# Moving attention scores inside a feed-forward unit of a two-layer graph network, with a new order of work at both ends

## The chip, the cores and the metric

The kernel runs on one core of a Trainium2 chip, in fp32. A core has TensorE for matrix products (PE in the profile; its weight loads are PEld), VectorE (DVE), ScalarE (ACT), GpSimd (POOL) and SyncE (SP), which here only issues transfers. Each engine works through its own queue in order. SBUF holds the data; TensorE writes its results to PSUM, from where VectorE and ScalarE read them. The metric is the time of the device in microseconds (us), lower is better. [...]

## What is computed

The input is x with 128 batches of 128 tokens by 256 features, and for each batch an adjacency matrix of zeros and ones. Two layers follow each other. Cut to what matters:

```python
# layer 0: attention with 8 heads, values chosen by the relation adj == r
attn = softmax(q @ k.T / sqrt(32))
out  = sum(attn * (adj == r) @ (src @ Wv[r]) for r in range(4))
x    = ln(src + out @ Wo)
x    = ln(x + gelu(x @ W1) @ W2)
# layer 1: two graph attention steps
def gat(h, W, a):
    Wh = h @ W
    e = leaky_relu(Wh @ a[:256] + (Wh @ a[256:]).T, 0.2)
    return softmax(where(adj > 0, e, -9e15), axis=1) @ Wh
h = ln(x + gat(gat(x, W1, a1), W2, a2))
h = ln(h + relu(h @ w_ff1) @ w_ff2)
```

Since adj holds only zeros and ones, the kernel needs two value projections: all exponentials times the values of relation 0, plus the exponentials that the adjacency leaves times the difference of the values of relation 1 and 0. Sums that it keeps on the way are checked at the end; if the check fails, a general pass repeats the work. It does not run here.

## The kernel before

**Groups.** The 128 batches are worked on in 32 groups of four (512 tokens). The loop over groups is software-pipelined: in iteration g the kernel is in the first feed-forward of group g+1, in the graph layer and the second feed-forward of group g, in the attention of group g+2 and in the projections of groups g+2 and g+3.

**Products.** The projections and the feed-forwards use a form of the 2x2 block product that needs seven products in place of eight. They are called B11, B21, B22 and T1 to T4; the sums of weights that they need are made once, by `combined` (L184), and those of the data by VectorE (`turned`, L389 to L392). A feed-forward (`ffn`) makes the hidden activations in two units, r=0 and r=1. In each, TensorE does T3, T2, B21, T1, T4, then B11 of the next unit if there is one, then B22, each four matmuls of L411. Products that share a sum accumulate in the same PSUM bank: `seeded` is held throughout and takes T2, T1 and B22 in turn, with what ScalarE or VectorE must read in between. So after T1 VectorE's addition L466 reads `seeded`, and B22 can only be written once it has. ScalarE applies GELU or ReLU (L435). Then follow the seven products with the second matrix, sixteen matmuls of L420 each: po1 (B11, copied to `seeded` by L498), po7 (T3), T2, B21, T1, T4 and B22. The projections (`projected`, products L641) use the banks `qa` and `qb`.

**Attention.** `scores` makes one pair of batches: 32 matmuls of 32 rows (L709) into four banks, for the first pair in the order `qa`, `qb` and the two banks of `ps_s`, and four exponentials of ScalarE (L715) that empty them. `masked` multiplies them with the adjacency on VectorE (L725). `sums` makes the denominators (`pden`, L742) and the value sums (`pav`, L756); ScalarE and VectorE turn them into `oT` (L766 to L778); `output` applies Wo (L791) and adds to x (`added`, L327).

**Graph layer.** `layer1` makes `wh` (L875), spreads one column of it over all partitions (`spread`: a transpose, and a write to HBM that is read back by all partitions, L838 and L839; for the first and last groups by matmuls, L828), and `edges` makes the weights `gs`: sums on ScalarE (L847), the leaky slope on VectorE (L851), exponentials (L853), adjacency and sums (L857), scaling (L864). Then come the products `py` (L888), the same once more, and `pg2` (L901).

**The order.** Nothing is scheduled by a planner. All stages are Python generators that `yield` between steps, and `in_order(...)` steps them: `(f1, 2)` takes two steps of the first feed-forward. Inside `tc.manual_schedule` every engine executes its instructions in the order in which they were written by these steps, and waits for what an instruction needs. In the lists f1 and f2 are the two feed-forwards, l1 the graph layer, at the attention, pr the projections, n0 to n3 the layer norms, `exp` and `gelu` the loads of ScalarE's function tables, `ahead` and `turned` the transposes. There are lists for the front (groups 0 and 1), for g=0, for the steady loop (g from 1, with small differences in the last iteration) and for the tail (the last group).

Of the kernel before, what the change touches and what calls it, by code (L numbers as in the profile page):

```python
# [10 lines left out]
F32 = mybir.dt.float32  # L11
# [13 lines left out]
P = 128  # L25
# [82 lines left out]
def fast_pass(ctx, tc, a, out):  # L108
# [73 lines left out]
    def combined(w):  # L182
        for o, p, q in ((T3, B22, T1), (T1, T1, B11), (T2, B22, T1), (T4, B21, T2)):
            nc.vector.tensor_sub(w[:, o], w[:, p], w[:, q])  # L184
# [508 lines left out]
    def scores(S, p):  # L693

        qT, kT = S["qT"], S["kT"]
        n = f"{S['g']}_{p}"


        banks = ((ps_1, "qa"), (ps_1, "qb"), (ps_s, "s"), (ps_s, "s"))
        pss = [  # L700
            pool.tile([P, 2, NCH, P], F32, tag=t, name=f"ps_{n}_{s}")
            for s, (pool, t) in enumerate(banks if p == 0 and S["g"] > 1 else banks[2:] + banks[:2])
        ]
        for u in range(2):
            bs = slice((2 * p + u) * P, (2 * p + u + 1) * P)
            for c in range(NCH):
                for s in range(HC):
                    rs = slice(s * DH, (s + 1) * DH)
                    nc.tensor.matmul(  # L709
                        pss[s][:, u, c, :], kT[rs, c, bs], qT[rs, c, bs],  # L710
                        start=True, stop=True,
                    )
        S["e", p] = e = w1p.tile([P, HC, 2, NCH, P], F32, tag="e", name="e_" + n)
        for s in range(HC):
            nc.scalar.activation(e[:, s], pss[s], AF.Exp, scale=SCALE)  # L715
            if s == 1:
                yield

    def masked(S, p):
# [10 lines left out]
    def sums(S, p):  # L730


        e, pm = S["e", p], S["pm", p]
        n = f"{S['g']}_{p}"

        pool, tag = (ps_1, "fe") if S["g"] > 1 and p == 0 else (ps_s, "s")
        pden = pool.tile([P, 2, NCH, P], F32, tag=tag, name="pden_" + n)
        pav = ps_1.tile([P, 2, NCH, P], F32, tag="av", name="pav_" + n)

        def plain():  # L740
            for s in range(HC):
                nc.tensor.matmul(  # L742
                    pden[s * DH : (s + 1) * DH], k.ones, e[:, s], start=True, stop=True
                )


        late = S["g"] > 1
        if not late:
            plain()
        for u in range(2):  # L750
            v = S["v"][:, 2 * p + u]
            for c in range(NCH):
                for r, m in enumerate((e, pm)):
                    for s in range(HC):
                        d0 = r * D + c * P + s * DH
                        nc.tensor.matmul(  # L756
                            pav[s * DH : (s + 1) * DH, u, c, :],
                            v[:, d0 : d0 + DH], m[:, s, u, c, :],
                            start=(r == 0), stop=(r == 1),
                        )  # L760
        if late:
            plain()

        g, oT = S["g"], S["oT"]
        rd = w1p.tile([P, 2, NCH, P], F32, tag="rd", name="rd_" + n)
        nc.scalar.activation(  # L766
            rd, pden, AF.Identity, accum_out=c_att[:, 1, g, p : p + 1]
        )
        nc.scalar.activation(
            pden, pden, AF.Relu, bias=k.lo, scale=-1.0, accum_out=c_att[:, 0, g, p : p + 1]  # L770
        )
        yield
        nc.vector.reciprocal(rd[:, 0], rd[:, 0])
        yield
        nc.vector.reciprocal(rd[:, 1], rd[:, 1])
        for u in range(2):
            bs = slice((2 * p + u) * P, (2 * p + u + 1) * P)
            nc.vector.tensor_mul(oT[:, :, bs], pav[:, u], rd[:, u])  # L778
        yield

    def attention(S):

        n = str(S["g"])
        S["oT"] = oT = w1p.tile([P, NCH, T], F32, tag="oT", name="oT_" + n)

        def output(p):
            po = mm_tile(f"pwo_{n}_{p}")
            for s in range(2):
                b = 2 * p + s
                for c in range(NCH):  # L790
                    nc.tensor.matmul(  # L791
                        po[:, s * D : (s + 1) * D], oT[:, c, b * P : (b + 1) * P], wo[:, c, :],
                        start=(c == 0), stop=(c == NCH - 1),
                    )
            added(S, 0, p, po)

        for p in range(G // 2):
            late = S["g"] > 1
            if p == 0 or not late:
                parts = scores(S, p)  # L800
                next(parts)
                if p == 0:
                    yield
                next(parts, None)
                yield
            masked(S, p)
            yield
            rest = sums(S, p)
            next(rest)
            yield  # L810
            if p == 0 and late:
                parts = scores(S, 1)
                next(parts)
                yield
                next(parts, None)
                yield
            yield from rest
        for p in range(G // 2):
            output(p)
            yield  # L820
# [87 lines left out]
    def store(S, bs=slice(0, G)):  # L908
        t0 = S["g"] * T
        nc.sync.dma_start(  # L910
            out[t0 + bs.start * P : t0 + bs.stop * P, :].rearrange("(b p) d -> p b d", p=P),
            S["x"][:, bs],
        )
# [23 lines left out]
    with tc.manual_schedule(engines={ET.PE, ET.Activation, ET.DVE, ET.SP, ET.Pool}):  # L937
# [11 lines left out]
        def output_bias():  # L949
# [7 lines left out]
            prepared(first)  # L957

        in_order(
            (pr, 4), (at, 2), (pr, 2), at, (pr, 2), (at, 4), (pr1, 2),  # L960
            at, output_bias, at, (pr1, 2), (at, 3), pr1, at, (at1, 2), n0, n0, lambda: combined(w1), pr1, at1, lambda: turned(first, 0), (at1, 2),
        )
        f1 = first_ffn(first)
        prepared(S1)
        st[2] = entered(2)
        pr = projected(st[2])
        in_order(
            gelu, (f1, 4), lambda: combined(w2), pr1, f1, f1, at1, at1, f1, lambda: combined(wqk), pr1, lambda: combined(wv), f1, n0, at1, (f1, 2), n0, f1, at1,
            (f1, 3), gwu, at1, f1, gwu, f1, at1, gwu,
            f1, at1, f1, gwu, at1, f1, n0_, pr, n0_, (f1, 4), n1_, (pr, 5), lambda: turned(S1, 0),  # L970
        )
        for g in range(NG - 1):
            S, S1 = st[g], st[g + 1]
# [9 lines left out]
            if g == 0:  # L983
                l1 = layer1(S)
                in_order(
                    f1, n1_, lambda: combined(u1), lambda: combined(u2), (pr, 2), (f1, 3), lambda: turned(S, 1), (pr, 2), f1, (n0_, 2), f1, l1, f1, (n1_, 2), l1, l1, f1, l1,
                    (f1, 2), (l1, 2), (pr, 2), f1, l1, (pr, 2), f1, pr, l1, f1, l1, f1, (l1, 2), exp, f1, (at, 2), (l1, 2),
                )
            else:
                n3 = norm(st[g - 1], 3)  # L990
                in_order(
                    pr, lambda: turned(S1, 0), (pr, 2), *(() if more else (f2_,)), f1, l1, gelu, (pr, 2), f2_, n3, f1, l1, pr,
                    n0_, f1, (pr, 2), (f1, 3), n0_, l1, f1, (pr, 2), l1, f1, n3, (pr, 2), f1, l1, f1, n3, (pr, 2),
                    (f1, 3), n3, lambda: store(st[g - 1]), f1, (n1_, 2), exp, (at, 2), f1, (l1, 3),
                )
            in_order(
                f1, (pr, 2), l1, f1, (pr, 2), at, f1, (pr, 2), l1, n2, (pr, 2), f1, n2, (pr, 2), f1, (pr, 2), f1, (pr, 2), *((ahead,) if more else ()), (at, 2), f1, n1,
                *(() if more else (ahead,)),
            )
            if not more:  # L1000
# [12 lines left out]
        in_order(f2, n1, (f2, 2), lambda: turned(S1, 1))  # L1013
        l1 = layer1(S1)
        in_order(
            f2, l1, f2, (l1, 2), f2, l1, (f2, 2), (l1, 2), n1, (f2, 2), l1, n1, f2, l1, f2, l1, f2, l1, n2, f2, (l1, 3), n2,
            (f2, 3), l1, (f2, 2), l1,
        )
        n2, n3 = norm(S1, 2), norm(S, 3)
        in_order(n2, f2, n2, (f2, 3), lambda: turned(S1, 2))  # L1020
        f2 = second_ffn(S1)
        in_order(f2, n3, (f2, 3), n2, n3, (f2, 4), n2, n3, (f2, 4), n3, lambda: store(S), (f2, 2))
        checks()
# [3 lines left out]
        normed(S1, 3, pair(1))  # L1027
        in_order(f2)
        root(S1, 3, pair(0))
        for p in (1, 0):  # L1030
            if p == 0:
                normed(S1, 3, pair(0))
            for step in range(2):
                scaled(S1, 3, step, (p,))
            store(S1, pair(p))

    same = flat(w1p.tile([P, G, P], F32, tag="gs", name="same"))[:, : NG * G * 2]
    fin = c_out.rearrange("p g b s -> p (g b s)")  # L1040
    nc.vector.tensor_tensor(same, fin, fin, op=ALU.is_equal)
    good = k.tile([P, 3], "good")
    nc.vector.tensor_reduce(good[:, 0:1], same, AX.X, ALU.min)
    nc.vector.tensor_reduce(good[:, 1:2], ok, AX.X, ALU.min)
    nc.vector.tensor_mul(good[:, 2:3], good[:, 0:1], good[:, 1:2])
    pf = mm_tile("pflag")
    nc.tensor.matmul(pf[:1, :1], good[:, 2:3], k.ones[:, 0:1], start=True, stop=True)
    bad = k.tile([1, 1], "bad", I32)
# [332 lines left out]
```

## Time and profile before

The median of three runs is 2760.3 us (2760.15 to 2761.74); the profiled span is 2759.6 us.

| engine | busy us | share of the span | instructions |
|---|---|---|---|
| PE | 2717.9 | 98% | 21621 |
| PEld (overlaps PE) | 2374.0 | 86% | 21621 |
| DVE | 2285.9 | 83% | 5320 |
| ACT | 1608.6 | 58% | 3589 |
| POOL | 135.9 | 5% | 137 |

The page has this table, the chain of work that ended last and the costliest groups of instructions. The windows view gives for a stretch of time its length, the busy time and count of each engine, the TensorE clock that was granted (PEclk, 1.00 is full), the share of the transfer engines and GB/s. A line of the timeline view gives the start in us, the duration, the engine, the line of code, the operation, the tile written, the tiles read, the shapes and how many instructions are joined in the line; in square brackets stands how long the engine had been idle, and what released it. Matmuls overlap, so a line of sixteen matmuls has a duration somewhat longer than its distance to the next start. The repeating part has a period of 82.8 us.

### The profile page before, as it was taken

Reading aid. Unit: us, or ns where it says so; the run is one execution under the profiler, and the core shown is the slowest. Engines: PE = TensorE matmul, PEld = TensorE weight load, DVE = VectorE, ACT = ScalarE, POOL = GpSimd, SP = SyncE. Lnnn points to the kernel's source line nnn. Section 1 sums busy time; section 2 is a strip of 40 time slices with the busy share of each in tenths; the row PEclk is TensorE's granted clock in tenths of the full one; section 3 lists DMA queues with packets and bytes.
Section 4 is the critical chain, followed back from the end, with each engine's and each line's share of the span. In section 5 each row is a group of like instructions: output and inputs, shape, how many; then the busy total and the mean of one; then the engine's idle time right before and its main releaser. Section 6 shows DMA issues by size and latency. Waiting matters only on the chain.

```text
span 2759.6 us, 54205 instructions
## 1 busy us (share of the span) xinstructions
PE 2717.9 (98%) x21621; PEld 2374.0 (86%) x21621; DVE 2285.9 (83%) x5320; ACT 1608.6 (58%) x3589; POOL 135.9 (5%) x137
## 2 busy tenths in 40 slices
PE   8899999999999999999999999999999999999997
PEld 5788898888888888888888888888888889888876
DVE  5778888888888888888888888888888888888866
ACT  4556656556556556565566565565665665655653
POOL 0000000000000000000000000000000000000000
PEclk9999999999999999999999999999999999999999
DMA  6001010010101010100101010101001101001000
GB/s 178 1 24 36 32 35 17 24 36 32 36 16 35 25 35 32 35 16 24 36 32 36 17 34 24 36 32 36 16 28 32 36 32 31 21 24 36 13 12 17
DMA packets 70234, 86.12 MB, mean 31 GB/s; under 512 B 8428, under 2 KB 48728, under 8 KB 69976
## 3 DMA queue, kind: packets, MB, share of 16 engines
q1 hardware_dynamic: 68872, 82.20, 9.6%
q8 instruction: 172, 2.82, 0.4%
q14 instruction: 86, 0.70, 0.1%
q10 hardware_dynamic: 1104, 0.40, 0.1%
HBM read 65.68 MB, written 16.90 MB: 30 GB/s over the span
## 4 chain that ended last, share of the span: by engine, by line
PE 94%; DVE 3%; ACT 2%; issue 0%; POOL 0%; ACTq 0%; POOLq 0%; DVEq 0%
PE po L420 16%; PE ph L411 15%; PE seeded L411 13%; PE seeded L420 12%; PE pav L756 4%; PE pwo L791 4%; PE pw L875 4%; PE pqqa L641 4%; PE pvqa L641 4%; PE pt L300 3%; PE pvqb L641 3%; PE pqqb L641 3%; PE ps L709 3%; PE py L888 2%; PE pden L742 2%; PE pg L901 2%
## 5 line engine op out<-in xcount | busy, mean ns | idle before, releaser
L349 ACT ACTIVATE x<-x,sh,rs 128x256 f32<-128x256 f32 x388 | 202.9, 608 | 425.8 <-DVE sh L344 425.8
L335 POOL TENSOR_TENSOR rs<-rs,mhalf 128x4 f32<-128x4 f32 x129 | 133.4, 1034 | 2571.8 <-DVE rs L334 2322.7
L411 PE MATMUL seeded<-yS,w_L_gnn_w_ff 128*128 128x256 f32 x768 | 207.2, 392 | 2.2 <-ACT seeded L483 2.2
L466 DVE TENSOR_TENSOR hT<-seeded,p 128x512 f32<-128x512 f32 x128 | 88.5, 692 | 142.2 <-ACT hT L435 82.4
L411 PE MATMUL seeded<-yS,w_L_gnn_W 128*128 128x256 f32 x768 | 201.3, 384 | 3.2 <-ACT seeded L483 2.2
L411 PE MATMUL ph<-yT,w_L_gnn_w_ff 128*128 128x256 f32 x768 | 203.5, 388 | 0.4 <-ACT yT L303 0.4
L411 PE MATMUL ph<-yT,w_L_gnn_W 128*128 128x256 f32 x768 | 197.4, 379 | 0.4 <-ACT yT L303 0.4
L320 DVE BATCH_NORM_STATS2 st<-x 128x6 f32<-128x256 f32 x512 | 192.2, 417 | 6.7
L411 PEld LDWEIGHTS seeded<-yS,w_L_gnn_w_ff 128*128 128x128 f32 x768 | 137.8, 189 | 66.5 <-issue 25.1
L420 PE MATMUL po<-w_L_gnn_W,hT 128*128 128x128 f32 x1536 | 190.0, 277 | 0.0
L420 PEld LDWEIGHTS po<-w_L_gnn_W,hT 128*128 128x128 f32 x1536 | 183.9, 192 | 6.7
L420 PE MATMUL po<-w_L_gnn_w_ff,hT 128*128 128x128 f32 x1536 | 187.0, 275 | 0.0
L420 PEld LDWEIGHTS po<-w_L_gnn_w_ff,hT 128*128 128x128 f32 x1536 | 184.1, 192 | 3.3
L411 PEld LDWEIGHTS seeded<-yS,w_L_gnn_W 128*128 128x128 f32 x768 | 138.0, 190 | 40.3 <-DVE hT L466 12.2
L411 PEld LDWEIGHTS ph<-yT,w_L_gnn_W 128*128 128x128 f32 x768 | 145.6, 190 | 20.7 <-ACT yT L303 0.7
L411 PEld LDWEIGHTS ph<-yT,w_L_gnn_w_ff 128*128 128x128 f32 x768 | 141.1, 190 | 23.3 <-ACT yT L303 1.1
L725 DVE TENSOR_TENSOR pm<-e,adj 128x512 f32<-128x512 f32 x256 | 159.1, 683 | 0.0
L435 ACT ACTIVATE hT<-hT,c_L_gnn_b 128x256 f32<-128x256 f32 x256 | 109.5, 498 | 51.4 <-DVE hT L466 49.5
L715 ACT ACTIVATE e<-ps 128x512 f32<-128x512 f32 x256 | 133.9, 591 | 5.6 <-PE ps L709 5.6
L435 ACT ACTIVATE hT<-hT,c_L_gnn_b_ff 128x256 f32<-128x256 f32 x256 | 110.7, 524 | 32.8 <-DVE hT L466 29.1
L847 ACT ACTIVATE gs<-spread,wh 128x128 f32<-128x128 f32 x120 | 38.4, 390 | 155.6 <-DMA spread<-hbm 155.6
L420 PEld LDWEIGHTS seeded<-w_L_gnn_W,hT 128*128 128x128 f32 x1024 | 124.3, 192 | 3.5 <-DVE hT L517 0.2
(196 smaller groups left out, 6500.8 us busy)
## 6 DMA issues: line engine op xcount, KB each, us to landing
xT<-in_xT_dram SPq DMA_DIRECT2D x32, 512.0 KB, 6.2
x<-in_x_dram SPq DMA_DIRECT2D x32, 512.0 KB, 5.1
out_dram<-x SPq DMA_DIRECT2D x31, 512.0 KB, 2.9
spread<-hbm SPq DMA_DIRECT2D x59, 256.0 KB, 3.1
adj<-in_adjT_dram SPq DMA_DIRECT2D x32, 256.0 KB, 4.2
w_L_gnn_W<-in_L_gnn_W_dram SPq DMA_DIRECT2D x8, 256.0 KB, 6.2
w_L_gnn_w_ff<-in_L_gnn_w_ff_dram SPq DMA_DIRECT2D x8, 256.0 KB, 4.9
hbm<-line SPq DMA_DIRECT2D x59, 2.0 KB
```

Source lines behind the costliest of these rows:

```text
L320: nc.vector.bn_stats(st[:, b % 2, :], S["x"][:, b, :])
L335: nc.gpsimd.tensor_tensor(rs[:, bs], rs[:, bs], k.mhalf[:, bs], op=ALU.pow)
L349: nc.scalar.activation(x[:, b, :], x[:, b, :], AF.Identity, bias=sh[:, b : b + 1], scale=rs[:, b : b + 1],)
L411: nc.tensor.matmul(bank[:, s * TH : (s + 1) * TH], wa[:, form, 0, f * P : (f + 1) * P], m, start=start and s == 0, stop=True, skip_group_c ...
L420: nc.tensor.matmul(bank[:, s * P : (s + 1) * P], m[:, f, s * P : (s + 1) * P], wb_[:, form, f, :], start=start and s + f == 0, stop=True, ...
L435: nc.scalar.activation(o[:, s], o[:, s] if src is None else src[:, s * TH : (s + 1) * TH], func, bias=ba[:, f : f + 1],)
L641: nc.tensor.matmul(bank[:, s * TH : (s + 1) * TH], *ops, start=start and s == 0, stop=True, skip_group_check=True,)
L715: nc.scalar.activation(e[:, s], pss[s], AF.Exp, scale=SCALE)
L725: nc.vector.tensor_mul(pm[:, s], S["e", p][:, s], S["ad"][:, pair(p), None, :].to_broadcast([P, 2, NCH, P]),)
L756: nc.tensor.matmul(pav[s * DH : (s + 1) * DH, u, c, :], v[:, d0 : d0 + DH], m[:, s, u, c, :], start=(r == 0), stop=(r == 1),)
L791: nc.tensor.matmul(po[:, s * D : (s + 1) * D], oT[:, c, b * P : (b + 1) * P], wo[:, c, :], start=(c == 0), stop=(c == NCH - 1),)
L875: nc.tensor.matmul(pw[:, :NU], yT[:, c, b * P : (b + 1) * P], wu[:, c, :], start=(c == 0), stop=(c == NCH - 1),)
```

## The change

It has four parts; the matmuls and their number stay what they are.

1. **Scores.** In the steady lists, the scores' matmuls of the first pair stand between the products T4 and B22 of unit r=1 of the first feed-forward, where they stood behind B22. To allow this, `scores` yields for the first pair after its matmuls, and then writes all four exponentials in one step.
2. **Exponentials and value products.** These exponentials come behind the copy of po1 and the edges' sums L847 in ScalarE's queue (they stood ahead of both). The first two value products of the projections (`pvqa`, `pvqb`, which need the banks that the exponentials empty) come one product of the second matrix later.
3. **Front.** The scores and sums of group 0 come closer together, the projections of group 1 later; the second scores of group 1 come before the first feed-forward of group 0, where they stood inside it, between two uses of GELU; the sums of weights for later stages are made later, and so are the norm's scalings in the list of g=0. Groups 0 and 1 change the banks of `pden`, and group 1 follows the late order of the sums that the later groups have.
4. **Tail.** In the last iteration and the last list the graph layer comes earlier against the norms and the second feed-forward; two products of the second matrix are put around the last transposes; and the reductions of the final check come ahead of the last scaling of the output.

```diff
@@ -711,9 +711,11 @@
                         start=True, stop=True,
                     )
         S["e", p] = e = w1p.tile([P, HC, 2, NCH, P], F32, tag="e", name="e_" + n)
+        if p == 0:
+            yield
         for s in range(HC):
             nc.scalar.activation(e[:, s], pss[s], AF.Exp, scale=SCALE)
-            if s == 1:
+            if p and s == 1:
                 yield
 
     def masked(S, p):
@@ -733,7 +735,7 @@
         e, pm = S["e", p], S["pm", p]
         n = f"{S['g']}_{p}"
 
-        pool, tag = (ps_1, "fe") if S["g"] > 1 and p == 0 else (ps_s, "s")
+        pool, tag = (ps_1, "fe") if p == 0 else (ps_s, "s")
         pden = pool.tile([P, 2, NCH, P], F32, tag=tag, name="pden_" + n)
         pav = ps_1.tile([P, 2, NCH, P], F32, tag="av", name="pav_" + n)
 
@@ -795,7 +797,7 @@
             added(S, 0, p, po)
 
         for p in range(G // 2):
-            late = S["g"] > 1
+            late = S["g"] > 0
             if p == 0 or not late:
                 parts = scores(S, p)
                 next(parts)
@@ -957,17 +959,18 @@
             prepared(first)
 
         in_order(
-            (pr, 4), (at, 2), (pr, 2), at, (pr, 2), (at, 4), (pr1, 2),
-            at, output_bias, at, (pr1, 2), (at, 3), pr1, at, (at1, 2), n0, n0, lambda: combined(w1), pr1, at1, lambda: turned(first, 0), (at1, 2),
+            (pr, 4), (at, 3), (pr, 2), (at, 5), (pr, 2), at, output_bias, pr1, (at, 3), pr1, at, n0, (pr1, 3), (at1, 2), n0,
+            lambda: combined(w1), pr1, at1, lambda: turned(first, 0), (at1, 4),
         )
         f1 = first_ffn(first)
         prepared(S1)
         st[2] = entered(2)
         pr = projected(st[2])
         in_order(
-            gelu, (f1, 4), lambda: combined(w2), pr1, f1, f1, at1, at1, f1, lambda: combined(wqk), pr1, lambda: combined(wv), f1, n0, at1, (f1, 2), n0, f1, at1,
+            gelu, (f1, 2), at1, at1, pr1, pr1, (f1, 4), at1, f1, f1, n0, lambda: combined(w2), f1,
+            f1, n0, f1,
             (f1, 3), gwu, at1, f1, gwu, f1, at1, gwu,
-            f1, at1, f1, gwu, at1, f1, n0_, pr, n0_, (f1, 4), n1_, (pr, 5), lambda: turned(S1, 0),
+            f1, at1, f1, gwu, lambda: combined(wqk), at1, f1, n0_, pr, n0_, (f1, 4), n1_, (pr, 5), lambda: turned(S1, 0),
         )
         for g in range(NG - 1):
             S, S1 = st[g], st[g + 1]
@@ -983,18 +986,19 @@
             if g == 0:
                 l1 = layer1(S)
                 in_order(
-                    f1, n1_, lambda: combined(u1), lambda: combined(u2), (pr, 2), (f1, 3), lambda: turned(S, 1), (pr, 2), f1, (n0_, 2), f1, l1, f1, (n1_, 2), l1, l1, f1, l1,
-                    (f1, 2), (l1, 2), (pr, 2), f1, l1, (pr, 2), f1, pr, l1, f1, l1, f1, (l1, 2), exp, f1, (at, 2), (l1, 2),
+                    f1, n1_, lambda: combined(u1), lambda: combined(u2), (pr, 2), (f1, 3), lambda: turned(S, 1),
+                    (pr, 2), f1, f1, l1, f1, l1, l1, f1, (n0_, 2), l1, (f1, 2), (l1, 2), (pr, 2), f1, l1, (pr, 2), f1, pr,
+                    lambda: combined(wv), l1, f1, l1, (n1_, 2), f1, (l1, 2), exp, f1, (at, 2), (l1, 2),
                 )
             else:
                 n3 = norm(st[g - 1], 3)
                 in_order(
                     pr, lambda: turned(S1, 0), (pr, 2), *(() if more else (f2_,)), f1, l1, gelu, (pr, 2), f2_, n3, f1, l1, pr,
                     n0_, f1, (pr, 2), (f1, 3), n0_, l1, f1, (pr, 2), l1, f1, n3, (pr, 2), f1, l1, f1, n3, (pr, 2),
-                    (f1, 3), n3, lambda: store(st[g - 1]), f1, (n1_, 2), exp, (at, 2), f1, (l1, 3),
+                    f1, *(() if more else (l1,)), (f1, 2), at, n3, lambda: store(st[g - 1]), f1, (n1_, 2), exp, f1, *((l1,) if more else ()), at, (l1, 2),
                 )
             in_order(
-                f1, (pr, 2), l1, f1, (pr, 2), at, f1, (pr, 2), l1, n2, (pr, 2), f1, n2, (pr, 2), f1, (pr, 2), f1, (pr, 2), *((ahead,) if more else ()), (at, 2), f1, n1,
+                f1, l1, f1, (pr, 2), f1, (pr, 2), at, (pr, 2), l1, n2, (pr, 2), f1, n2, (pr, 2), f1, (pr, 2), f1, (pr, 2), *((ahead,) if more else ()), (at, 2), f1, n1,
                 *(() if more else (ahead,)),
             )
             if not more:
@@ -1013,11 +1017,10 @@
         in_order(f2, n1, (f2, 2), lambda: turned(S1, 1))
         l1 = layer1(S1)
         in_order(
-            f2, l1, f2, (l1, 2), f2, l1, (f2, 2), (l1, 2), n1, (f2, 2), l1, n1, f2, l1, f2, l1, f2, l1, n2, f2, (l1, 3), n2,
-            (f2, 3), l1, (f2, 2), l1,
+            f2, l1, f2, (l1, 3), f2, l1, f2, l1, f2, l1, (f2, 3), l1, n2, f2, l1, n2, f2, l1, n1, f2, n1, (l1, 2), f2, (l1, 2), (f2, 2), l1,
         )
         n2, n3 = norm(S1, 2), norm(S, 3)
-        in_order(n2, f2, n2, (f2, 3), lambda: turned(S1, 2))
+        in_order(n2, f2, n2, (f2, 2), lambda: turned(S1, 2), (f2, 2))
         f2 = second_ffn(S1)
         in_order(f2, n3, (f2, 3), n2, n3, (f2, 4), n2, n3, (f2, 4), n3, lambda: store(S), (f2, 2))
         checks()
@@ -1027,22 +1030,22 @@
         normed(S1, 3, pair(1))
         in_order(f2)
         root(S1, 3, pair(0))
+
+        same = flat(w1p.tile([P, G, P], F32, tag="gs", name="same"))[:, : NG * G * 2]
+        fin = c_out.rearrange("p g b s -> p (g b s)")
+        nc.vector.tensor_tensor(same, fin, fin, op=ALU.is_equal)
+        good = k.tile([P, 3], "good")
+        nc.vector.tensor_reduce(good[:, 0:1], same, AX.X, ALU.min)
+        nc.vector.tensor_reduce(good[:, 1:2], ok, AX.X, ALU.min)
+        nc.vector.tensor_mul(good[:, 2:3], good[:, 0:1], good[:, 1:2])
         for p in (1, 0):
-            if p == 0:
+            scaled(S1, 3, 0, (p,))
+            if p:
                 normed(S1, 3, pair(0))
-            for step in range(2):
-                scaled(S1, 3, step, (p,))
+            scaled(S1, 3, 1, (p,))
             store(S1, pair(p))
 
 
-
-    same = flat(w1p.tile([P, G, P], F32, tag="gs", name="same"))[:, : NG * G * 2]
-    fin = c_out.rearrange("p g b s -> p (g b s)")
-    nc.vector.tensor_tensor(same, fin, fin, op=ALU.is_equal)
-    good = k.tile([P, 3], "good")
-    nc.vector.tensor_reduce(good[:, 0:1], same, AX.X, ALU.min)
-    nc.vector.tensor_reduce(good[:, 1:2], ok, AX.X, ALU.min)
-    nc.vector.tensor_mul(good[:, 2:3], good[:, 0:1], good[:, 1:2])
     pf = mm_tile("pflag")
     nc.tensor.matmul(pf[:1, :1], good[:, 2:3], k.ones[:, 0:1], start=True, stop=True)
     bad = k.tile([1, 1], "bad", I32)
```

## The prediction

> **What bounds the kernel now.** I read the page first, then the windows view by stage, then the timeline of TensorE over one steady iteration, and last the timelines of front and tail.
>
> ```profile
> PE 2717.9 (98%) x21621; PEld 2374.0 (86%) x21621; DVE 2285.9 (83%) x5320; ACT 1608.6 (58%) x3589; POOL 135.9 (5%) x137
> PE 94%; DVE 3%; ACT 2%; issue 0%; POOL 0%; ACTq 0%; POOLq 0%; DVEq 0%
> ```
>
> TensorE is busy for 98% of the span and 94% of the chain that ended last. The number of matmuls does not change (21621), so only gaps between them and slow stretches can be won. The windows view says where these are:
>
> ```profile
> 0.00:100.00 100.00, 90.19 (x728) 64.40 (x729) 65.07 (x134) 42.74 (x86) 3.52 (x9) 0.98 0.44 123
> 900.00:1000.00 100.00, 99.90 (x790) 88.96 (x788) 86.45 (x210) 53.95 (x120) 5.15 (x5) 1.00 0.10 30
> 2680.00:2725.00 45.00, 39.11 (x227) 32.74 (x225) 28.91 (x80) 20.95 (x49) 2.32 (x2) 0.96 0.00 1
> ```
>
> In the middle TensorE looks full (99.90 of 100); the front lacks 10 us and the tail 6. But "busy" hides small losses, since matmuls overlap. So I took the distance from one start to the next in the timeline, here at the place that the change touches:
>
> ```profile
> 974.75 1.03 PE L411 MATMUL seeded<-yS,w_L_gnn_W 128*128 128x256 f32 x4
> 975.62 1.03 PE L411 MATMUL ph<-yT,w_L_gnn_W 128*128 128x256 f32 x4
> 976.63 1.13 PE L411 MATMUL seeded<-yS,w_L_gnn_W 128*128 128x256 f32 x4
> 977.70 1.17 PE L709 MATMUL ps<-qT,kT 32*128 32x128 f32 x32
> 978.80 2.05 PE L420 MATMUL po<-w_L_gnn_W,hT 128*128 128x128 f32 x16
> 980.69 0.50 PE L420 MATMUL po<-w_L_gnn_W,h 128*128 128x128 f32 x3
> ```
>
> The rows are T1, T4, B22, the scores, then products B11 and T3 of the second matrix. Where nothing is waited for, four matmuls of L411 take 0.87 us (974.75 to 975.62; 0.863 in the finer records), and sixteen of L420 take 1.79 (2705.05 apart, 2706.93 to 2708.72 in the tail). Here T4 to B22 takes 1.01, B22 to the scores 1.07, and po1 1.89.
>
> **What the skill says.** "TensorE: Matmul & The Clock Gate", section "Step-by-step: what each phase is for": weight loads are pulled ahead of matmuls in flight, so a stream of matmuls hides its loads. The trace agrees by its exception: B22, which waited, has 1.13 for 1.03, so about 0.10 of its first load is exposed. Section "What's actually happening" of the same page: after an idle window of about 3.4 us, free-running, the clock halves. The trace has a clock of 0.55 and 0.60 at 29 to 33 us, after 2 us with 0.35 busy; where the window falls it doesn't show. "ScalarE: Activation LUTs", section "What ACT_TABLE_LOAD costs": about 1.28 us for the load; the trace has 1.28 at 66.33 and at 70.69.
>
> **The steady iteration.** Period 82.8 us; attention exists for groups 2 to 31 and the edited list runs from g=1, so 29 iterations have all of it. On TensorE one block moves: the scores go from behind B22 to between T4 and B22. Two value products move by one unit of the second feed-forward matrix, at the same cost.
>
> Before: B22 cannot start until VectorE's addition after T1 (L466), which reads the same bank:
>
> ```profile
> 975.89 0.69 DVE L466 TENSOR_TENSOR hT<-seeded,p 128x512 f32<-128x512 f32 x1 [1.12 <-ACT hT L435]
> ```
>
> It ends at 976.58, and B22 starts at 976.63. The losses: 0.15 (T4 to B22: 1.01 less 0.863), 0.10 (B22's exposed load), 0.09 (change into 32-row scores, the rest of B22's 1.07), 0.10 (exposed load behind the scores, po1's 1.89 less 1.79): 0.45. After: the scores start at about 976.58 (q and k are there by 975) and take 1.10 to 977.68. The addition has ended by then, so T4's 0.15 goes, and B22 follows at once. The change into the scores (0.09) stays, now behind T4; one exposed load (0.10) stays, now on B22; po1 follows a like product and loses nothing. 0.20 in all: 0.45 − 0.20 = 0.256 per iteration, times 29 = **7.4 us**. Lower bound: if loads pay again behind B22, 0.15 × 29 = 4.4.
>
> Now what could take it back. B22's activation is 0.62 later (978.85 to 979.66); queued behind it in ScalarE are the table load (1.28), now the `seeded` copy L498 and the edges' sums L847 ahead of the four exponentials.
>
> ```profile
> 979.06 1.28 ACT L537 ACT_TABLE_LOAD   x1
> 980.46 2.00 ACT L715 ACTIVATE e<-ps 128x512 f32<-128x512 f32 x4
> 982.37 0.36 ACT L498 COPY seeded<-po 128x256 f32<-128x256 f32 x1
> 982.67 1.27 ACT L847 ACTIVATE gs<-spread,yh 128x128 f32<-128x128 f32 x4
> 983.97 0.69 DVE L851 SCALAR_TENSOR_TENSOR gs<-gs 128x512 f32<-128x512 f32 x1 [1.06 <-ACT gs L847]
> ```
>
> The copy moves from 982.37 to about 981.1, ends 981.4; T2, which needs it, starts at 982.2 (slack 0.8). L847 runs 981.4 to 982.65; its broadcast, issued at 974.81, lands after about 3.2 us at 978.0, so it does not wait (slack 3.4). The exponentials run 982.6 to 984.6. They release the score banks; the first value product needs bank qa, free at about 983.15, and now starts at 984.0 because it was put one unit later (slack 0.85). Without that delay it would have wanted the bank at 982.2 and waited 0.9. The edges' exponential L853 ends at 985.1 where it ended at 985.32. VectorE's L851 moves from 983.97 to 982.9 and the edges end near 987.2; the second graph product wants them at 988.4 (slack 1.2). The masks end at 990.9, and their product starts near 999.9. So all of this is hidden, the tightest by 0.8.
>
> **The front.** The first pair's score exponentials of group 0 hold TensorE:
>
> ```profile
> 28.96 5.40 PE L579 MATMUL pq<-xT,w_qk 128*128 128x512 f32 x8 [1.65 <-ACT e L715]
> 29.00:31.00 2.00, 2.00 (x3) 0.94 (x4) 2.00 (x5) 0.39 (x1) 0.00 (x0) 0.55 0.86 264
> ```
>
> After, what follows those scores is a value product that needs only the first exponential: 1.65 becomes about 0.65 (−1.0). The eight 512-wide projections that follow at half clock take 5.24 from start to next start, where the next such eight take 3.54: −1.7, if the shorter wait keeps the clock. A wait at 44.9 to 47 (0.09, and scores at 2.52 for 1.10) shrinks by 1.5, and a new one of about 1.1 stands ahead of the second output product, whose input VectorE multiplies late: −3.1 by the transposes at 51. Then the value sums of group 1 wait about 2.2 for masks queued behind an addition that waits for the norm on ScalarE; 1.0 of it the transposes wait already (they take 2.77 from 51.17 where eight take 0.87): +1.2. In the first feed-forward the second scores of group 1 go, and with them two table loads, since the change puts those scores ahead of it:
>
> ```profile
> 65.67 1.13 PE L411 MATMUL ph<-yT,w_L_gnn_W 128*128 128x256 f32 x4
> 68.27 1.99 PE L590 MATMUL pv<-w_v,xT 128*128 128x256 f32 x8 [1.47 <-ACT e L715]
> 73.48 1.13 PE L411 MATMUL seeded<-yS,w_L_gnn_W 128*128 128x256 f32 x4 [1.49 <-ACT seeded L483]
> ```
>
> The products at 65.67 and 70.97 take 2.60 and 2.52 for 0.86 (1.74 and 1.65 lost), and the masked value sums at 76.64 lose 1.6 (1.82 for seven that take 0.2): 5.0, less about 0.7 for waits of those scores in their new place: −4.3. A later T2 loses 1.0 to `seeded` (+1.0). In the g=0 list, the first graph product's wait of 1.86 goes because VectorE's scalings (2 × 1.28) and the weight sums move out of its way; those sums cost 0.3 twice elsewhere: −1.25. Sum: −3.1 + 1.2 − 4.3 + 1.0 − 1.25 = −6.45. Another half-clock piece of 1.7 has some chance of one in four around 50, where TensorE waits: I take **−6**, bounds −2 (the half clock stays and waits come back) and −9.
>
> **The tail.**
>
> ```profile
> 2691.86 1.13 PE L411 MATMUL seeded<-yS,w_L_gnn_w_ff 128*128 128x256 f32 x4 [1.49 <-ACT seeded L483]
> 2695.35 1.14 PE L888 MATMUL py<-wh,gs 128*128 128x258 f32 x4 [1.50 <-DVE gs L864]
> 2717.79 0.33 PE L300 MATMUL pt<-ident,x 128*128 128x128 f32 x1 [1.82 <-ACT x L349]
> ```
>
> The last group's edges go ahead of the scalings and of h3 on VectorE: the 1.50 at 2695.35 and 0.15 beside it go (−1.65). The copy at 2691.86 gains 0.45. The graph product of 2710.51 is moved ahead, and of the second-matrix products (1.79 each) T4 goes ahead of the last transposes and B22 behind them. There TensorE loses 1.98 ahead of the first transpose, 1.95 in the eight and 0.92 in the next product (1.78 for 0.86, the clock lowered): 4.85 in all, of which the norm that it waits for, started sooner, leaves some 1.85: −3.0. The final check (equality and two minima) goes ahead of the last scaling, into VectorE's idle time; the additions that it stood behind now end sooner: −0.33. 1.65 + 0.45 + 3.0 + 0.33 = **−5.4**, bounds −2 and −7. A wait of 1.6 for VectorE ahead of group 30's graph sum stays.
>
> **Sum.** −7.4 − 6.0 − 5.4 = −18.8; 2760.3 − 18.8 = 2741.5.
>
> **Rivals.** (a) Steady gain lost: loads and the change of form cost as much in the new place, or a buffer wait of 0.25 appears; front and tail alone: 2760.3 − 11.4 = 2748.9. For: every slack was computed with hand-moved times. Against: 0.15 of it is a plain wait for L466, covered by 1.10 of scores. (b) The front gives back: half clock near 50 and the new waits (1.1, 1.9) in full, so −1 instead of −6: 2746.5. For: the clock window's phase is unknown. (c) Slower: the exponentials now stand behind L847, which waits for a DMA. By the waits view such waits come 30 times, up to 5.7 us; the page's groups have them:
>
> ```profile
> L847 ACT ACTIVATE gs<-spread,wh 128x128 f32<-128x128 f32 x120 | 38.4, 390 | 155.6 <-DMA spread<-hbm 155.6
> ```
>
> If the broadcast came 5 us late here, past its slack of 3.4, the banks would be free 1.6 late, 0.75 beyond their slack, plus a late mask: near 0.8 net each iteration, 0.8 × 29 − 11.4 = +11.8, some 2772. Against: all of it is in the form `spread,wh`, the first graph step; the one behind the scores is `spread,yh`, which shows no such wait.
>
> **Numbers.** Forecast 65%, (a) 18%, (b) 12%, (c) 5%. The range 2735 to 2751 holds the forecast's bounds and most of (a) and (b). Faster 0.92, same 0.03, slower 0.05.
>
> **What would show it.** Right: period 82.5; in TensorE's timeline T4, ps, B22, po with ps to B22 at 1.1, B22 to po below 1.0 and po 1.79; L847 ahead of the exponentials with no DMA wait; no table load in 60 to 75; clock 1.00 near 29 to 33; 2695's wait gone. Wrong: a releaser `ACT e L715` at pvqa, or a period of 82.8 or more.

## The result and the profile after

The changed kernel takes 2742.2 us (median; 2741.5 to 2743.03) where the kernel before takes 2760.4 (2760.15 to 2761.74) beside it: 18.2 us less, ratio 0.9933, 95% interval 0.9916 to 0.9950. The forecast was 2741.5, range 2735 to 2751.

Lines below the edit in `scores` are two higher in the changed kernel: L849 is L847 of before, L717 is L715, L853 is L851. First the page's busy times, then the windows view (length, busy time and count of each engine, clock, transfer share, GB/s) for the front, a steady stretch and the tail:

```profile
PE 2705.4 (99%) x21621; PEld 2374.2 (87%) x21621; DVE 2282.8 (83%) x5320; ACT 1610.6 (59%) x3587; POOL 135.6 (5%) x137
0.00:100.00 100.00, 92.01 (x760) 67.40 (x760) 68.24 (x148) 42.48 (x90) 4.27 (x10) 1.00 0.45 123
900.00:1000.00 100.00, 99.90 (x853) 87.49 (x853) 84.86 (x199) 60.26 (x133) 6.16 (x6) 1.00 0.12 38
2660.00:2705.00 45.00, 41.23 (x246) 34.80 (x247) 29.56 (x84) 25.27 (x58) 2.84 (x3) 1.00 0.00 1
```

The number of matmuls is the same and TensorE's busy time is 12.5 us lower: losses that counted as busy have gone. ScalarE has two instructions fewer, the two table loads in the first feed-forward. In the steady stretch the windows view cannot tell the two kernels apart: 99.90 in both. The chain view of this run ends after its first step, at the last addition on VectorE, and answers nothing here. TensorE's timeline at the place of the change does:

```profile
965.38 1.03 PE L411 MATMUL seeded<-yS,w_L_gnn_W 128*128 128x256 f32 x4
966.24 1.03 PE L411 MATMUL ph<-yT,w_L_gnn_W 128*128 128x256 f32 x4
967.20 1.17 PE L709 MATMUL ps<-qT,kT 32*128 32x128 f32 x32
968.30 1.13 PE L411 MATMUL seeded<-yS,w_L_gnn_W 128*128 128x256 f32 x4
969.27 1.95 PE L420 MATMUL po<-w_L_gnn_W,hT 128*128 128x128 f32 x16
971.05 1.95 PE L420 MATMUL po<-w_L_gnn_W,h 128*128 128x128 f32 x16
```

Start to start: T4 0.96 (0.863 and the change into 32 rows), scores 1.10, B22 0.97 (0.863 and one exposed load), po1 1.78. Nothing waits for L466 any more (its line below): it ends at 967.20, and B22, which may write the bank only after it, starts at 968.30, when the scores are through. The four rows took 1.01 + 1.07 + 1.10 + 1.89 = 5.07 before and take 4.81 now: 0.26. The iteration's period says the same: from the transposes at 243.10 to those at 2595.61 before (28 iterations) it is 84.02, from 235.68 to 2581.06 after it is 83.76. (The period of 82.8 given above is wrong, and so are the 82.5 and 82.8 among the signs of being right or wrong: they stand for 83.76 and 84.02. No step of the sum uses them.) ScalarE and VectorE beside it:

```profile
966.51 0.69 DVE L466 TENSOR_TENSOR hT<-seeded,p 128x512 f32<-128x512 f32 x1 [1.13 <-ACT hT L435]
970.32 1.28 ACT L537 ACT_TABLE_LOAD   x1
971.73 0.36 ACT L498 COPY seeded<-po 128x256 f32<-128x256 f32 x1
972.03 1.27 ACT L849 ACTIVATE gs<-spread,yh 128x128 f32<-128x128 f32 x4
973.21 2.00 ACT L717 ACTIVATE e<-ps 128x512 f32<-128x512 f32 x4
973.45 0.69 DVE L853 SCALAR_TENSOR_TENSOR gs<-gs 128x512 f32<-128x512 f32 x1
```

Copy, edges' sums and exponentials follow the table load without a gap; none waits for the broadcast. The first exponential ends near 973.8, and the value product that needs its bank (a PSUM tile of 128 by 512 values) starts at 974.62 in the full timeline: a slack, or time to spare, of 0.8, as worked out.

### The profile page after: what moved, and what is told of

It is laid out like the page before. It is cut to its first block, busy times and chain, and to the rows that moved or that the text cites. A ratio compares the mean times of both kernels' runs of the same rounds, so it can differ in the third digit from the quotient of the medians.

```text
span 2740.1 us, 54262 instructions
## 1 busy us (share of the span) xinstructions
PE 2705.4 (99%) x21621; PEld 2374.2 (87%) x21621; DVE 2282.8 (83%) x5320; ACT 1610.6 (59%) x3587; POOL 135.6 (5%) x137
## 3 DMA queue, kind: packets, MB, share of 16 engines
q8 instruction: 172, 2.82, 0.4%
## 5 line engine op out<-in xcount | busy, mean ns | idle before, releaser
L466 DVE TENSOR_TENSOR hT<-seeded,p 128x512 f32<-128x512 f32 x128 | 88.5, 692 | 140.9 <-ACT hT L435 83.5
L717 ACT ACTIVATE e<-ps 128x512 f32<-128x512 f32 x256 | 134.2, 593 | 6.2 <-PE ps L709 4.0
L435 ACT ACTIVATE hT<-hT,c_L_gnn_b 128x256 f32<-128x256 f32 x256 | 109.6, 500 | 45.0 <-DVE hT L466 44.9
L849 ACT ACTIVATE gs<-spread,wh 128x128 f32<-128x128 f32 x120 | 38.5, 392 | 154.1 <-DMA spread<-hbm 154.1
```

Source lines behind the costliest of these rows:

```text
L435: nc.scalar.activation(o[:, s], o[:, s] if src is None else src[:, s * TH : (s + 1) * TH], func, bias=ba[:, f : f + 1],)
L466: nc.vector.tensor_add(hidden(1, 1, r), halves(seeded), halves(p7))
L849: nc.scalar.activation(s[:, b, :], target[:, b, :], AF.Identity, bias=source[:, b, :])
```

## The experiments

Times are medians, each beside runs of the kernel before on the same chip (2760.7 to 2761.5 there), with the ratio to it and its 95% interval.

The diffs show the lists as they are in the steady iterations, without the conditions for the last one.

**Each part alone.** `steady_only` has the new steady lists and, for group 3 on, the new yield in `scores`; front, g=0 and tail are as before.

```diff
+        early = p == 0 and S["g"] > 2
+        if early:
+            yield
...
-                    (f1, 3), n3, lambda: store(st[g - 1]), f1, (n1_, 2), exp, (at, 2), f1, (l1, 3),
+                    f1, (f1, 2), at, n3, lambda: store(st[g - 1]), f1, (n1_, 2), exp, f1, l1, at, (l1, 2),
```

> The kernel before with the steady lists of the change alone (g from 1 to 29: scores between T4 and B22, exponentials behind the edges' sums, value products a unit later); front, list of g=0 and tail as before. Theory (gain by removing the wait for L466 and one exposed weight load): 0.25 us in each of 29 iterations, so about 2760.4 - 7.2 = 2753.2. Rival (a steady gain is not there, all of it is front and tail): 2760 +- 1. Rival (exponentials behind the broadcast hold the banks): over 2765.

Measured: 2753.9, ratio 0.9973 (0.9962 to 0.9985), 7.6 less than before. In the trace the lead over before grows from 1.01 at the transposes of 243 to 8.22 at those of 2596: 7.21 over 28 iterations, 0.2575 in each, as 0.256 said. So rival (a) and the broadcast rival are out.

`front_only` has the new lists for the front and g=0 and the bank and late order of groups 0 and 1.

```diff
-            late = S["g"] > 1
+            late = S["g"] > 0
...
-            (pr, 4), (at, 2), (pr, 2), at, (pr, 2), (at, 4), (pr1, 2),
+            (pr, 4), (at, 3), (pr, 2), (at, 5), (pr, 2), at, output_bias, pr1, (at, 3), pr1, at, n0, (pr1, 3), (at1, 2), n0,
...
```

> The kernel before with the front lists, the list of g=0 and the bank and order of the sums of groups 0 and 1 of the change; steady lists and tail as before. Theory (parts are independent, since TensorE is the bound between them): 7.2 less, by the distance that the two traces have at the transposes of 159 us, so about 2753.2. Rival (the steady part or the tail gives a front gain back, for instance at a transfer): 2756 or more.

Measured: 2754.3, ratio 0.9974 (0.9964 to 0.9985), 7.1 less. From the first transposes of the steady part to the end the trace keeps a lead of 7.2 within 0.3, counted from the first projection.

`tail_only` has the new lists of the last iteration, of the tail, and the check's new place.

```diff
-            f2, l1, f2, (l1, 2), f2, l1, (f2, 2), (l1, 2), n1, (f2, 2), l1, n1, f2, l1, f2, l1, f2, l1, n2, f2, (l1, 3), n2,
-            (f2, 3), l1, (f2, 2), l1,
+            f2, l1, f2, (l1, 3), f2, l1, f2, l1, f2, l1, (f2, 3), l1, n2, f2, l1, n2, f2, l1, n1, f2, n1, (l1, 2), f2, (l1, 2), (f2, 2), l1,
```

> The kernel before with the last iteration's lists, the tail lists and the place of the final check of the change; all else as before. Theory: 5.0 less, about 2755.4; the final check by itself gives none of it (its 0.33 was not seen in the trace of the whole change). Rival (the tail gain is only a shorter path because the groups before ended sooner): 2759 or more.

Measured: 2755.8, ratio 0.9979 (0.9970 to 0.9988), 5.6 less. The three parts sum to 0.27 + 0.26 + 0.21 = 0.74% where the whole change has 0.67% (0.50 to 0.84): within the intervals they add up.

**What makes the steady gain.** `scores_back` puts only the score matmuls back behind B22; ScalarE's order and the late value products stay.

```diff
-f1, (f1, 2), at, n3, lambda: store(st[g - 1]), f1, (n1_, 2), exp, f1,
+f1, (f1, 2), n3, lambda: store(st[g - 1]), f1, at, (n1_, 2), exp, f1,
```

> The changed kernel with the 32 score matmuls alone put back behind B22 in the steady lists; exponentials behind the edges' sums and value products late, as in the change. Theory (the whole steady gain is TensorE's order, the moves on ScalarE and of the value products only make it possible): 0.25 in 29 iterations comes back, 2742.2 + 7.3 = 2749.5. Rival (part of the gain is on ScalarE, as edges' weights that come sooner): 2742 to 2747.

Measured: 2749.8, ratio 0.9958 (0.9945 to 0.9972). Three lines of its timeline:

```profile
969.63 1.13 PE L411 MATMUL seeded<-yS,w_L_gnn_W 128*128 128x256 f32 x4
970.69 1.17 PE L709 MATMUL ps<-qT,kT 32*128 32x128 f32 x32
971.79 2.05 PE L420 MATMUL po<-w_L_gnn_W,hT 128*128 128x128 f32 x16
```

B22 takes 1.06 from start to start, as before the change, the scores 1.10 and po1 1.89. The period is 84.01, that of the kernel before within 0.01, and the median is 7.6 above the changed kernel's 2742.2: the whole steady gain is gone with the matmuls' place. The moves on ScalarE bring nothing by themselves. What they are for, the next two show.

`exps_ahead` puts the exponentials ahead of the copy and the edges again:

```diff
-f1, (n1_, 2), exp, f1, l1, at, (l1, 2),
+f1, (n1_, 2), exp, at, f1, l1, (l1, 2),
```

> The changed kernel with the four exponentials put ahead of the copy of po1 and of the edges' sums in ScalarE's queue again (scores still between T4 and B22). Theory: in the changed kernel the table load and its activation end at 971.73; four exponentials end at 973.73, the copy at 974.1, and the product T2, which starts at 972.84 there, waits 1.25 and pays a load of 0.1: 1.35 in 29 iterations, 2742.2 + 39 = 2781, slower than before. Rival (the order on ScalarE is of no weight, since it is busy for 59% only): 2742 +- 3.

Measured: 2779.9, ratio 1.0068 (1.0053 to 1.0084): slower than before. Its timeline, ScalarE and TensorE:

```profile
984.11 2.00 ACT L717 ACTIVATE e<-ps 128x512 f32<-128x512 f32 x4
986.02 0.36 ACT L498 COPY seeded<-po 128x256 f32<-128x256 f32 x1
986.43 2.05 PE L420 MATMUL seeded<-w_L_gnn_W,h 128*128 128x128 f32 x16 [1.04 <-ACT seeded L498]
```

TensorE stands idle for 1.04 ahead of the product T2, until the copy behind the exponentials is done. Its period is 1.29 longer than the changed kernel's; 1.35 was worked out.

`values_early` lets the first two value products stand where they were:

```diff
-                f1, l1, f1, (pr, 2), f1, (pr, 2), at, (pr, 2), l1, n2,
+                f1, (pr, 2), l1, f1, (pr, 2), at, f1, (pr, 2), l1, n2,
```

> The changed kernel with the first two value products at their old place, one product of the second matrix sooner. Theory (the first exponential, 973.21 to 973.7, is what frees bank qa): the value product would be due at 972.84 and starts at about 973.8, 0.95 plus a load of 0.1 in 29 iterations, 2742.2 + 30 = 2772. Rival (the slack of the bank is larger than worked out): 2742 +- 3.

Measured: 2773.9, ratio 1.0048 (1.0033 to 1.0063).

```profile
982.86 2.00 ACT L717 ACTIVATE e<-ps 128x512 f32<-128x512 f32 x4
983.48 1.13 PE L641 MATMUL pvqa<-w_v,xT 128*128 128x256 f32 x4 [0.83 <-ACT e L717]
```

The value product waits for the first exponential to empty bank `qa`, 1.09 in each iteration. So neither move is a gain, and with either one left out the changed kernel, gains of front and tail included, is 12 to 18 slower than before.

**The table loads of the front.** `scores_in_ffn` puts the second scores of group 1 back inside the first feed-forward.

```diff
-            lambda: combined(w1), pr1, at1, lambda: turned(first, 0), (at1, 4),
+            lambda: combined(w1), pr1, at1, lambda: turned(first, 0), at1,
...
-            gelu, (f1, 2), at1, at1, pr1, pr1, (f1, 4),
+            gelu, (f1, 2), (at1, 5), pr1, pr1, (f1, 4),
```

> The changed kernel with the second scores of group 1 put back inside the first feed-forward of group 0, behind its T3, so that ScalarE loads the table of Exp and then that of GELU again there. Theory (table loads and the waits around them are the largest part of the front's gain): +4.3 less 0.5 to 1 that the changed kernel waits for those scores itself, so 2745.5 to 2746.5. Rival (the front's gain is elsewhere, in the clock and in the order of the projections): 2742 to 2743.5.

Measured: 2747.6, ratio 0.9953 (0.9938 to 0.9968), 5.4 above the changed kernel's median, which is from other runs. Some 1.7 of the 5.4 go with the mean clock that each run lists: the profiled run, with 0.999 like all runs of the changed kernel, took 2746.0, the other three, with 0.997 and 0.998, took 2746.9 to 2748.5. In the traces, counted from the first projection, it is 3.2 later at the transposes of 101 us (97.41 for 94.22), and nothing changes after that. So the table loads and their waits are worth 3.2, somewhat less than the 3.3 to 4.3 expected, and more than half of the 5.5 that the front saves at full clock (table below).

**A better version.** The steady losses that are left were 0.27 and 0.10 at the start of the first feed-forward, where the query product T2 waits for ScalarE's copy of the first query product, queued behind two transposed copies. `q_first` takes that copy, and then T2, ahead:

```diff
-                    pr, lambda: turned(S1, 0), (pr, 2), *(() if more else (f2_,)), f1, l1, gelu, (pr, 2), f2_, n3, f1, l1, pr,
+                    (pr, 2), lambda: turned(S1, 0), (pr, 3), *(() if more else (f2_,)), f1, l1, gelu, f2_, n3, f1, l1, pr,
```

> The changed kernel with one more edit in the steady lists, for the largest wait that is left there (0.27 behind the first product of the first feed-forward and 0.10 for an exposed load, waiting for ScalarE's copy of the first query product behind two transposed copies): that copy goes ahead of the transposes' copies, and the query product T2 ahead of the feed-forward's first product. Theory: 0.25 to 0.37 less in 29 iterations, so 2731.5 to 2735. Rival (the feed-forward's T2 then waits for the copy to seeded, or the transposes' copies come too late): 2740 to 2745.

Measured: 2767.1, ratio 1.0023 (1.0013 to 1.0033): slower than before, and 25 above the changed kernel, a miss. The old wait is gone, but its timeline has a new one a few products later, ahead of the feed-forward's T1:

```profile
1045.52 1.28 ACT L537 ACT_TABLE_LOAD   x1
1048.11 0.56 ACT L460 COPY p<-seeded 128x512 f32<-128x512 f32 x1
1048.72 1.13 PE L411 MATMUL seeded<-yS,w_L_gnn_W 128*128 128x256 f32 x4 [0.85 <-ACT p L460]
```

T1 needs the copy L460, which stands behind the load of the GELU table, another copy and a query copy. The query product between the feed-forward's B11 and T3 had been giving ScalarE the time for these, by the two timelines; the edit had been worked out for the copy to `seeded` alone. `q_first2` uses a pause on ScalarE for the query copy and puts the table load behind L460:

```diff
-                    (pr, 2), lambda: turned(S1, 0), (pr, 3), *(() if more else (f2_,)), f1, l1, gelu, f2_, n3, f1, l1, pr,
-                    n0_, f1, (pr, 2), (f1, 3), n0_,
+                    (pr, 2), lambda: turned(S1, 0), (pr, 4), *(() if more else (f2_,)), f1, l1, *(() if more else (gelu,)), f2_, n3, f1, l1,
+                    n0_, f1, *((gelu,) if more else ()), pr, f1, pr, (f1, 2), n0_,
```

> q_first with ScalarE's queue mended: there the wait had gone from the first product, and 1.02 us had come behind the product B21, whose follower T1 waited for the copy of seeded (L460), queued behind the load of the GELU table (1.28) and the copy of the second query product. Now that query copy (L660) comes ahead of the copy to seeded, in a pause that q_first had at 1043.06 to 1044.39, and the table load comes behind L460, directly ahead of the first GELU. Theory: the copies end near 1046.7 where T1 is due at 1047.7, so the 1.02 and the 0.10 behind it go; of the changed kernel's 0.37 at this place 0.10 is left (T2 waits for seeded): 0.27 in 28 to 29 iterations, 2742.2 - 7.6 = 2734.6. Rival (the GELU that comes 0.5 to 1.1 later holds bank fa or VectorE's additions): 2738 or more.

Measured: 2737.3, ratio 0.9913 (0.9899 to 0.9926). Between the transposes of 236 and 2581 it gains 7.26 on the changed kernel, 0.26 an iteration; the median has only 5 of the 7.6. Most of the rest goes with the clock: the profiled run, with a mean clock of 0.999, took 2735.0, one with 0.998 took 2734.8, and three with 0.997 or 0.998 took 2.2 to 3.2 more than the profiled one, while all runs of the changed kernel have 0.999. At which place the three met a lower clock isn't known, since they have no trace.

`exps_late` moves the last two exponentials of the second pair behind the norm and the first ReLU of the second feed-forward:

```diff
                 next(parts)
                 yield
+                if S["g"] > 1:
+                    yield from rest
                 next(parts, None)
...
-                f2, (at, 2), (f2, 2), n1, at, (f2, 3), lambda: turned(S1, 1), f2, at,
+                f2, at, (f2, 2), n1, at, f2, at, (f2, 2), lambda: turned(S1, 1), f2, at,
```

> The changed kernel with the last two exponentials of the second pair moved behind the norm and the first ReLU of the second feed-forward in ScalarE's queue, so that the copies for T2 and T1 of its first unit are no longer behind them. Theory: in the changed kernel B21 waits 0.14 and T1 0.10 there; these go, the masks are set by VectorE (it begins them at 1000.92) and end within 0.2 of before: 0.2 to 0.24 in 28 iterations, 2735.5 to 2737. Rival (the masks or the later ReLUs come too late and the value sums wait): 2742 or more.

Measured: 2739.5, ratio 0.9921 (0.9907 to 0.9935): about half of what was expected. The wait ahead of T1, the product behind B21, was 0.14 and is 0.03 in the trace; the 0.10 of exposed load that the expectation had added to it is still there, though hardly anything is waited for. The gain is 0.11 in each iteration.

`both_more` has the last two diffs together.

> Both edits of q_first2 and exps_late together on the changed kernel. Theory: they are 25 us apart in each iteration and add up: 2742.2 - 7.6 - 6.2 = 2728.4. Rival (one gives back what the other gains): no lower than the lower of the two.

Measured: 2731.6, ratio 0.9893 (0.9878 to 0.9908). Its steady stretch in the windows view:

```profile
900.00:1000.00 100.00, 100.00 (x852) 87.78 (x852) 85.10 (x197) 62.66 (x138) 5.16 (x5) 1.00 0.11 38
```

It is the fastest of all, 10.6 below the changed kernel; the profiled spans, 2729.9 and 2740.1, agree. Its iteration is 0.37 shorter than that of the changed kernel, about the sum of the two (0.26 and 0.11). That it stays 3.2 above the 2728.4 expected is the missing half of `exps_late`.

## Why the prediction was right

**Steady iteration: right in mechanism and size.** Predicted 0.45 of losses becoming 0.20, 0.256 saved; measured 0.254 by the period of the whole change and 0.2575 by `steady_only`. That the wait for L466 needs no engine to be faster, only something else to do meanwhile, is shown by `scores_back`. The slacks (0.8 for the copy, 0.85 for bank `qa`) were the part with the greatest risk, and two runs price them: without the order on ScalarE 1.29, without the late value products 1.09. Rival (a) is refuted. Rival (c) did not occur: the waits for the broadcast are the other graph step's alone also after the change, 154.1 us over 30. But a slower outcome was near in another form: the half-made changes are 12 to 18 slower than before.

**Front: the total was right, in part by luck; of its terms several were not.** −6 was predicted, −7.1 measured, so rival (b) is out. `tail_only` has the old front and ran it at full clock, `front_only` the new one; both counted from their first projection (7.38 and 7.47):

| stretch | predicted without clock | old front | new front | difference |
|---|---|---|---|---|
| to the first transposes | −1.0 − 1.5 + 1.1 = −1.4 | 42.64 | 42.96 | +0.3 |
| to the first feed-forward, with the scores' 1.10 left out | +1.2 | 6.23 | 6.27 | 0.0 |
| to the transposes of about 101 to 105, with the scores' 1.10 in both | −4.3 + 1.0 = −3.3 | 48.98 | 45.03 | −3.95 |
| to those of about 152 to 158 | −1.25 | 52.72 | 50.80 | −1.9 |
| sum | −4.75 | 150.57 | 145.06 | −5.5 |

The 1.65 that became 0.65 did so (the scores' stretch is 2.82 and becomes 1.84), and the new 1.1 ahead of the second output product came (1.09). The step "a wait at 44.9 to 47 shrinks by 1.5" failed: the scores there still take 2.64 for 1.10, since they now wait 0.50 for VectorE's addition L595 where they had waited 0.37 for L327, and the product behind them waits 0.49 for the exponentials as before. The step "+1.2", that the value sums of group 1 wait for masks, failed too: that stretch is unchanged. The two nearly cancel, which is luck. The third row came out 0.65 better: behind the scores' new place 0.43 is lost where 0.7 had been allowed, and the later T2 loses 0.83 where 1.0 had been; the rest was not traced. The last row was mis-sized: the 1.86 went as predicted, and the 0.6 for weight sums elsewhere did not come.

The step with the half clock needs a correction of its kind. Predicted: −1.7, as if the old front had to pay it. Windows of the old front in three runs, of the kernel before, of `tail_only` and of `steady_only`:

```profile
29.00:33.00 4.00, 4.00 (x6) 1.68 (x7) 2.62 (x5) 0.80 (x2) 0.00 (x0) 0.57 0.85 218
```

```profile
29.00:33.00 4.00, 3.50 (x8) 1.63 (x9) 3.17 (x7) 1.62 (x3) 0.00 (x0) 1.00 1.03 311
```

```profile
52.00:56.00 4.00, 4.00 (x55) 2.79 (x57) 3.97 (x9) 2.76 (x6) 0.00 (x0) 0.57 0.01 2
```

The same instructions with the same waits met half clock at 29 in one run, nowhere in another, and at 52 in a third, for a loss of 1.7, 0 and 1.2. The new front met it in none of nine traces. So this is a chance, not a fixed cost: the forecast counted the loss of one trace as certain, and that its −6 still came near −7.1 is in part luck. The twelve runs of `tail_only`, which has the old front, fit this: the six with a mean clock of 0.999 took 2754.2 to 2755.7, the six with 0.998 took 2755.9 to 2756.5. That the new front lowers the chance is likely by these traces (none of nine, against two of three) but not shown, and the lower mean clock in runs of `q_first2` says that a loss can still come somewhere in a kernel that has it.

In the windows view the clock is 0.50 from 29.18 to 32.59 in the kernel before and from 52.57 to 55.98 in `steady_only`, 3.41 us each time; in the 3.41 us ahead of these TensorE was busy for 1.76 and 2.29. That the same program meets it at different places agrees with what the Trainium skill says in "TensorE: Matmul & The Clock Gate", "What's actually happening", that the window is free-running. The page's idle window of about 3.4 us does not fit: the longest idle time of TensorE ahead of the two falls was 1.65 and 0.64, amid other gaps. What decides is open; `tail_only` waited as long (1.64) at the first of these places and kept its clock.

**Tail: right, a little smaller.** Predicted −5.4. `tail_only` shows the total; the terms are read from traces, and no run tries them one by one. From the transposes of the steady part's end to the start of the last full product it is 150.66 before and 145.71 after: −4.95. Two lines of the changed kernel's tail:

```profile
2679.05 1.14 PE L890 MATMUL py<-wh,gs 128*128 128x258 f32 x4 [0.21 <-DVE gs L866]
2691.42 1.99 PE L903 MATMUL pg<-yh,gs 128*128 128x256 f32 x8 [0.94 <-DVE gs L866]
```

The wait of 1.50 ahead of the first graph product is 0.21 (predicted 0), that ahead of the second, which had none, is 0.94, and behind it the 4.85 around the transposes is 0.73 (1.85 predicted). The lowered clock is gone: the products behind the transposes took 1.78 and 0.87 before and take 0.87 and 0.88; the other two kernels with the old tail had lost 1.4 there, all with the new tail nothing. The step "final check −0.33" failed: from the last full product to the end it is 13.29 before and 13.37 after. The last addition is indeed 0.2 sooner, but the first store is issued 0.7 later, since the check now stands ahead of it; that the store takes the gain away is argued and was not tried by itself.

**The sum.** It came within 0.7 of the measured 2742.2. The steady term and the tail carry this by their mechanism; the front's terms erred both ways and happened to balance. The range's upper end was a little tight against its own bounds: the three smallest gains, 4.4, 2 and 2, leave 2751.9, not 2751.

## What to carry to other kernels

A product that had to wait for another engine's read of its bank lost nothing to that wait once work that was ready stood between the two. The price of an order is to be read from start to start, since TensorE showed 99.90% busy here with and without the wait. Such a move paid only because what it delayed on the other engines had slack: go through each of their queues item by item, up to the next few products, before moving anything. The one step that was not gone through in that way (`q_first`) lost 25 us where the wait that it removed was worth 7.

## What the runs showed of the hardware that was not expected

A loss of half clock is a lottery even for one program: 1.7, 1.2 and 0 us in three traces of the same front, and the start varies by 1.3 us between the traces (first projection at 6.59 to 7.90 us, with the same instructions ahead of it). The Trainium skill, in "ScalarE: Activation LUTs", "What ACT_TABLE_LOAD costs", adds a drain of about 1.38 us to a load of 1.28. No such drain is seen here: the activation ahead of the load quoted above ends at 970.31, the load runs from 970.32 to 971.60, and the next activation starts at 971.62. And an exposed weight load of 0.10 on TensorE can stay after the wait that went with it has gone (B22 behind the scores, 1.13 and 0.97 to the next start; T1 in `exps_late`, 0.97 for 0.86).
